# TensorE's side and softplus steps ahead of the sum, in every unit of a state-space scan kernel

## The chip, the cores and the metric

One NeuronCore of a Trainium2 chip runs the whole program in one launch. The metric is device time in microseconds, from the start of the execution to its end; lower is better.

## The reference

The program is four layers of a two-dimensional selective scan ("ss2d") over x of shape (8, 48, 48, 96), each as `x = x + layer(group_norm(x))`. All layers have 192 inner channels, 16 states, four scan directions k, and L = 48 * 48 = 2304 positions. Cut to what matters here:

```python
xc, z = split(x @ in_proj_w.T)                    # 192 + 192 channels
xc = silu(depthwise_conv3x3(xc) + conv_b)
xs = [rows, columns, rows reversed, columns reversed] of xc
dts, Bs, Cs = split(einsum('bkdl,kcd->bkcl', xs, x_proj_w))
delta = softplus(dts @ dt_projs_w + bias)
# per direction and channel d, along l:
h = h * exp(delta * A[d, n]) + (delta * u) * B[n]     # 16 states n
y[d] = sum_n h[n] * C[n]
y = sum of the four directions, brought back to rows, + D * xs
y = layer_norm(y) * silu(z);  out = y @ out_proj_w.T
```

Layers 0 to 2 are this recurrence. Layer 3 is written in the reference as a cumulative sum with a decay and an epsilon; the kernel has a shorter path for it.

## The kernel before, in words

The batch is taken in four pairs of images. For each layer and pair there is a **prologue** (group norm, projection, convolution, the projections that give dt, B and C), a **scan** over 36 chunks, and an **epilogue** (layer norm, gate, output projection, residual). The epilogue of the pair before and the prologue of the pair after are cut into small *side steps* and run beside the scan.

A **chunk** is 768 positions of one of three channel tiles t, one of two layouts ph and one direction d. It is worked through in 16 **units**, one for each n; a unit holds two states of 64 channels, one on each half of the 128 partitions. Layers 0 to 2 have 3 * 4 * 36 * 16 = 6,912 units. What one unit n costs on each engine:

- SyncE's queue loads the row C of the state, spread over partitions, into `cb` (line 740, 9 buffers), four units ahead; for "pooled" states (n = 2, 5, 7, 10, 13, 15) also B into `bb` (3 buffers), five ahead.
- TensorE spreads B over the partitions into PSUM (`b`, line 678, 2 buffers) for the states that are not pooled. It does this for state n + 1 in unit n.
- ScalarE makes the decay `da = exp(dl * a)` (line 780), three units ahead, or for a pooled state into the PSUM buffer `b`, one ahead.
- VectorE multiplies `b` by `du` (line 810, not for pooled states) and scans (line 814).
- GpSimd multiplies the scan by C into `cb` (line 823) and, for pooled states, B by `du` (line 757), three units ahead.
- TensorE adds the products up over the states into `acc` (line 870). In unit n the *sum* of state n - 2 is issued (`LAG` = 2): the sum of an odd state waits for GpSimd's product of that state, the sum of an even state needs nothing newer. The last sum of a chunk falls into unit 2 of the next chunk; ScalarE then copies `acc` to `y` (`collect`, line 887) at the head of unit 3, and the first sum of the new chunk (`begin_sum`, line 855) waits for that copy. One chunk in six passes its `acc` on and isn't copied.

Beside the units runs `prepare`, the **softplus step** for the next chunk: delta = softplus(...) and `du` in two halves of 384 positions. It is a generator that `beside()` moves by one step per unit: in unit 15 of the chunk before (second half: unit 6) TensorE's dt matmuls (line 614); in 0 (7) ScalarE's Abs, Relu, Exp (lines 622 to 624); in 1 (8) Ln and two Identity (626 to 628); in 2 (9) and in 3 (10) eight TensorE matmuls each, which add up the parts (line 634); then in 4 (11) ScalarE's four copies to `dl` (line 589) and VectorE's product with u (642, 645; in unit 4 for the first half, in 12 for the second), and in 5 (13) four copies to `du` (589).

The order of each engine's instructions in layers 0 to 2 is the order in which the program writes them (`keep_order`). Engines wait for one another by semaphores. In unit n the program writes:

```python
busy = collected()          # ScalarE: y <- acc, if a sum ended in the unit before
get_ready(k + 1)            # loads; B of n + 1; decay of n + 3
catch_up()
c.scan(n)
...
if busy and l not in short:
    beside()                # softplus's step, one side step (none in unit 2)
... b.add_up(bn)            # the sum of state n - 2
if not (busy and l not in short):
    beside()
```

So before the change `beside()` stands ahead of the sum only in the 360 units 3 that begin with a copy of `acc`.

Of the kernel before, what the change touches and what calls it, by code (L numbers as in the profile page):

```python
# [103 lines left out]
def ss2d_layers_kernel(ctx: ExitStack, tc: tile.TileContext, x_in, consts, weights, out):  # L104
# [470 lines left out]
    def load_dt(c):  # L575
        r = layers[c.l].rank
        c.dts = sm1.tile([64, SCAN], F32, name="dts", tag="dts")
        for b in c.batches:
            q0 = 32 * b if c.t == 2 else 0
            nc.sync.dma_start(  # L580
                c.dts[q0 : q0 + r, : c.m],
                state[c.l, c.p]["xd"][c.ph, b, c.d * r : (c.d + 1) * r, c.c0 : c.c0 + c.m],
            )
# [101 lines left out]
    def store_some(n):  # L685
        for _ in range(min(n, len(late_stores))):
            o, z, at = late_stores.pop(0)
            nc.sync.dma_start(o[:, at], z[:, at])

    def collected():  # L690
        some = bool(late_sums)
        while late_sums:
            late_sums.pop(0)()
        return some

    def catch_up():
        while late_act:
            nc.scalar.copy(*late_act.pop(0))
# [450 lines left out]
    def drain(g):  # L1149
        for _ in g:  # L1150
            pass

    def step(g):
        next(g, None)
# [7 lines left out]
    def side_step(*sides):  # L1162

        for s in sorted(sides, key=lambda s: (not s.held, s.made / s.total)):
            got = next(s.g, s)
            s.held = got is True
            if got is not s and got is not GATED:
                s.made += 1
                return True
        return False  # L1170
# [3 lines left out]
    def mark():  # L1174
        marks.append(len(tc._region_blocks()[0].instructions))
# [15 lines left out]
    def run(pairs, short):  # L1191


        def units():
            for l, p in pairs:
                for gi, (t, ph, d) in enumerate(groups):
                    if l in short:
                        c = Edge(l, p, t, ph, d)
                        for i in range(NS // QUAD):
                            yield (l, p, gi * (NS // QUAD) + i), c, i  # L1200
                        continue
                    group = {}
                    for i in range(len(SCANS)):
                        c = Chunk(l, p, t, ph, d, i, group, c if d == 1 and i == 0 else None)
                        for n in range(NS):
                            yield (l, p, (gi * len(SCANS) + i) * NS + n), c, n

        def begin(l, p, first=False):
            if l not in layers:
                layers[l] = Layer(l)  # L1210
            return prologue(l, p, l in short, first)

        todo = list(units())

        def rest_of_sum(k):
            before = todo[k - 1][1] if k > 0 else None
            if isinstance(before, Chunk) and (k == len(todo) or todo[k][1] is not before):
                before.add_up(NS)

        def get_ready(k):  # L1220

            def early(ahead, what):
                for i in range(0 if k == 0 else k + ahead, min(k + ahead + 1, len(todo))):
                    getattr(todo[i][1], what)(todo[i][2])

            early(LOADS + 1, "load_b")
            early(LOADS, "load")
            if k == 0:
                todo[0][1].decay(todo[0][2])
            if k < len(todo):  # L1230
                (l, p, _), c, n = todo[k]
                if n == 0 and c.first and l not in short:
                    c.group["carry"] = capool.tile([P, NS], F32, name="carry", tag="carry")
                c.spread(n)
            early(DECAYS, "weigh")
            for i in range(k + DECAYS if k else 1, min(k + DECAYS + 1, len(todo))):
                todo[i][1].decay(todo[i][2])

        rest = begin(*pairs[0], first=True)
        while next(rest) is not READY:  # L1240
            pass
        rest = Side(rest)
        chunks = list(dict.fromkeys(c for _, c, _ in todo))
        drain(prepare(chunks[0]))
        behind = ahead = Side()
        coming = iter(())
        done = None
        mark()
        get_ready(0)
        for k, ((l, p, unit), c, n) in enumerate(todo):  # L1250
            at = pairs.index((l, p))
            following = pairs[at + 1] if at + 1 < len(pairs) else None
            if l in short and unit == 0:
                mark()
            per = NS // QUAD if l in short else NS
            all_units = len(groups) * (per if l in short else len(SCANS) * per)
            place["tiles"] = 3 * unit // all_units
            store_some(1)
            if done:
                behind, done = Side(epilogue(*done), 199), None  # L1260
            if unit == LAG and following:
                ahead = Side(begin(*following), 311)
            if k == 0:
                coming_to = 1
                coming = prepare(chunks[coming_to])
            if n == max(0, per - 1 - DECAYS):
                while coming_to < len(chunks) and not chunks[coming_to].ready:
                    next(coming)
            if n == 10 and coming_to + 1 < len(chunks):
                z = chunks[coming_to + 1]  # L1270
                if (z.l, z.p) == (l, p):
                    load_dt(z)
            busy = collected()
            get_ready(k + 1)
            catch_up()
            c.scan(n)
            if n == per - 1:
                drain(coming)
                if unit + 1 + per == all_units:
                    drain(behind.g)  # L1280
                    drain(ahead.g)
                coming_to = chunks.index(c) + 2
                coming = prepare(chunks[coming_to]) if coming_to < len(chunks) else iter(())


            def beside():
                step(coming)

                for _ in range(10 if l in short else 0 if ends else 1):
                    side_step(rest) or side_step(behind, ahead)  # L1290

            ends = l not in short and k > LAG and todo[k - LAG][2] == 0
            if busy and l not in short:
                beside()
            if k >= LAG:
                (bl, bp, _), b, bn = todo[k - LAG]
                rest_of_sum(k - LAG)
                if bl in short:
                    collected()
                b.add_up(bn)  # L1300
                if k > LAG and todo[k - LAG - 1][0][:2] != (bl, bp):
                    done = todo[k - LAG - 1][0][:2]
            if not (busy and l not in short):
                beside()
        for i in range(len(todo) - LAG, len(todo)):
            collected()
            rest_of_sum(i)
            todo[i][1].add_up(todo[i][2])
            catch_up()
        collected()  # L1310
        rest_of_sum(len(todo))
        collected()
        drain(epilogue(*pairs[-1]))

    last = NLAYER - 1
    run([(l, p) for l in range(NLAYER) for p in range(NPAIR)], (last,))

    keep_order(*marks[:2])
# [8 lines left out]
    with tc.If(nc.values_load(again, min_val=0, max_val=1) > 0):  # L1327
        run([(last, p) for p in range(NPAIR)], ())
# [95 lines left out]
```

## Time and profile before

| | |
|---|---|
| runs (median; lowest to highest) | 20210.51 us; 20204.88 to 20238.13 us (3 runs) |
| profiled execution | 20200.44 us; span of its instructions 20198.6 us; mean granted TensorE clock 0.908 |
| layers 0 to 2 | 0 to about 18,304 us of the span |
| layer 3 (short path) | about 18,304 to 20,198 us |
| busy in the whole span | PE 83%, VectorE (DVE) 87%, ScalarE (ACT) 80%, GpSimd (POOL) 88%, DMA queue 79% of 16 engines |
| busy in 5,000 to 6,000 us | PE 858, DVE 935, ACT 835, POOL 947 of 1000 us |
| one matmul of a sum, 128x384 f32 | 486 ns median; four records for one sum |
| one scan, 128x768 | 1,814 ns (`da`, with carry); one product on GpSimd 1,817 ns; one product on VectorE 946 ns |

How to read it: times are microseconds of one profiled execution unless marked ns. PE is TensorE's matmuls, PEld its weight loads, SPq the queue that issues DMAs. In a list of waits, "A <- B: x, n" says that A's engine sat idle for x us in all, n times, until B released it. In the timeline a line gives the start, the length, the engine, the source line, the tiles, and in brackets the idle time of the engine before it and who ended it. "issue" is idle time that the profile puts to nobody. VectorE and GpSimd are the fullest engines, and neither is full: the profile has to be read by who waits for whom.

### The profile page before, as it was taken

The numbers are of one execution on the slowest core, as the hardware profiler recorded it, in microseconds if no ns is written. First come the engines' busy times: TensorE is split into PE (matmuls) and PEld (weight loads), VectorE is DVE, ScalarE is ACT, GpSimd is POOL, SyncE is SP. The second block draws the span as 40 slices with busy tenths as digits, with TensorE's granted clock in tenths as the row PEclk, the third lists the DMA queues.
The fourth block names the chain that finished last, engine by engine and source line by source line (L and its number), as shares of the span: only waits on it lengthen the run. The fifth ranks groups of instructions, "written<-read, shape, count | busy, mean of one in ns | idle before, by whom it ended". The sixth has DMA issues, their size and how long they took to land.

```text
span 20198.6 us, 314848 instructions
## 1 busy us (share of the span) xinstructions
PE 16790.8 (83%) x92962; PEld 7792.6 (39%) x92962; DVE 17667.0 (87%) x14161; ACT 16224.6 (80%) x30014; POOL 17769.4 (88%) x10121
## 2 busy tenths in 40 slices
PE   7888887887888888888887888888888887888886
PEld 3333333333333333333333333333333333334565
DVE  6999998998999999999999999999999999996553
ACT  6777887887887887887887887877877887887786
POOL 6999999999999999999999999999999999995442
PEclk9998998998998998998998999998999998999997
DMA  5888888888888888888888888888888888884221
GB/s 157 231 224 223 226 222 221 227 223 220 225 226 224 224 231 224 223 228 223 225 228 223 223 225 226 223 226 221 221 224 222 222 225 221 220 222 117 79 74 50
DMA packets 2021150, 4200.80 MB, mean 208 GB/s; under 512 B 375920, under 2 KB 789360, under 8 KB 2017904
## 3 DMA queue, kind: packets, MB, share of 16 engines
q1 hardware_dynamic: 2019440, 4180.55, 79.2%
q8 instruction: 762, 12.48, 0.3%
q14 instruction: 948, 7.77, 0.2%
HBM read 4026.64 MB, written 152.27 MB: 207 GB/s over the span
## 4 chain that ended last, share of the span: by engine, by line
PE 21%; ACT 17%; DVE 14%; DMA 10%; issue 9%; POOL 3%; SPq 2%; DVEq 0%; POOLq 0%; ACTq 0%
DVE da L814 7%; PE acc L870 5%; PE ps L634 4%; DMA bb<-xd 4%; DVE b L810 4%; DMA cb<-xd 4%; ACT b L780 3%; ACT dl L589 3%; PE ps L314 2%; PE b L678 2%; ACT du L589 2%; POOL cb L823 2%; DVE bb L814 2%; ACT da L780 2%; SPq L740 1%
## 5 line engine op out<-in xcount | busy, mean ns | idle before, releaser
L823 POOL TENSOR_TENSOR cb<-cb,da 128x768 f32<-128x768 f32 x4320 | 7835.9, 1819 | 749.3 <-issue 253.1
L870 PE MATMUL acc<-cb,twin 128*64 128x384 f32 x27648 | 7200.8, 539 | 721.3 <-POOL cb L823 704.5
L814 DVE TENSOR_TENSOR_SCAN da<-da,carry,b 128x768 f32<-128x768 f32 x2880 | 5223.2, 1814 | 176.0 <-DVE b L810 0.9
L757 POOL TENSOR_TENSOR bb<-bb,du 128x768 f32<-128x768 f32 x2592 | 4716.9, 1820 | 222.2 <-DMA bb<-xd 125.6
L823 POOL TENSOR_TENSOR cb<-cb,bb 128x768 f32<-128x768 f32 x2592 | 4706.8, 1816 | 100.2 <-DVE bb L814 50.7
L810 DVE TENSOR_TENSOR b<-du,b 128x768 f32<-128x768 f32 x4320 | 4085.6, 946 | 690.2 <-PE b L678 604.2
L678 PE MATMUL b<-brow,pick 96*64 96x512 bf16 (+2 forms) x18816 | 2852.5, 353 | 1886.2 <-DVE da L814 1528.4
L780 ACT ACTIVATE da<-dl,a 128x768 f32<-128x768 f32 x4320 | 4011.3, 930 | 213.5 <-POOL cb L823 183.0
L870 PEld LDWEIGHTS acc<-cb,twin 128*64 128x64 f32 x27648 | 2452.5, 149 | 2998.4 <-POOL cb L823 1333.5
L814 DVE TENSOR_TENSOR_SCAN bb<-b,carry,bb 128x768 f32<-128x768 f32 x1728 | 3109.6, 1800 | 106.0 <-ACT b L780 35.6
L780 ACT ACTIVATE b<-dl,a 128x768 f32<-128x768 f32 x2592 | 2335.3, 901 | 623.2 <-DVE da L814 598.4
L678 PEld LDWEIGHTS <-pick 96*64 96x64 bf16 x18816 | 1077.9, 115 | 4164.4 <-DVE da L814 2717.6
L814 DVE TENSOR_TENSOR_SCAN da<-da,b 128x768 f32<-128x768 f32 x1440 | 2525.3, 1754 | 87.4 <-DVE b L810 1.4
L314 PE MATMUL ps<-pad,diag 128*64 128x480 f32 (+1 forms) x8640 | 2339.7, 567 | 34.6 <-ACT du L589 24.4
L589 ACT COPY dl<-ps 64x384 f32<-64x384 f32 x3456 | 1632.6, 472 | 697.9 <-PE ps L634 659.6
L589 ACT COPY du<-ps 64x384 f32<-64x384 f32 x3456 | 1633.5, 473 | 200.7 <-DVE ps L645 109.8
L634 PE MATMUL ps<-du,cst 128*64 128x384 f32 (+1 forms) x7296 | 1704.5, 506 | 76.5 <-ACT du L628 65.6
L814 DVE TENSOR_TENSOR_SCAN bb<-b,bb 128x768 f32<-128x768 f32 x864 | 1502.1, 1739 | 145.5 <-ACT b L780 92.2
L634 PE MATMUL ps<-dl,cst 128*64 128x384 f32 (+1 forms) x7296 | 1485.2, 483 | 0.0
L614 PE MATMUL ps<-dts,w 6*128 6x384 f32 (+5 forms) x2432 | 961.4, 605 | 205.0 <-DMA dts<-xd 105.4
L622 ACT ACTIVATE du<-ps,w 128x384 f32<-128x384 f32 (+1 forms) x912 | 519.9, 570 | 714.6 <-PE ps L614 701.0
L314 PEld LDWEIGHTS ps<-pad,diag 128*64 128x64 f32 x8640 | 751.8, 139 | 885.0 <-issue 729.6
(144 smaller groups left out, 19166.4 us busy)
## 6 DMA issues: line engine op xcount, KB each, us to landing
cb<-xd SPq DMA_DIRECT2D x13952, 192.0 KB
bb<-xd SPq DMA_DIRECT2D x5184, 192.0 KB
brow<-xb SPq DMA_DIRECT2D x864, 72.0 KB
ey<-yd SPq DMA_DIRECT2D x256, 216.0 KB
cb<-xd SPq DMA_DIRECT2D x128, 384.0 KB
yd<-y SPq DMA_DIRECT2D x216, 192.0 KB
ex<-xs SPq DMA_DIRECT2D x256, 108.0 KB
xb<-parts SPq DMA_DIRECT2D x96, 216.0 KB
```

The source lines that it names most:

```text
L314: nc.tensor.matmul(ps[half, :m], ly.diag[:, int(t == 2), j, half], pad[:, r0 + dy : r0 + dy + nr, dx : dx + W], start=(j == 0), stop=(j == 8),
L589: nc.scalar.copy(z[64 * h : 64 * h + 64, g, at], v[64 * g : 64 * g + 64])
L614: nc.tensor.matmul(o[:, :m], ly.dtw[q0 : q0 + r, k, chans], dts[q0 : q0 + r, at], start=True, stop=True,)
L622: nc.scalar.activation(e, v, AF.Abs, bias=bias)
L634: nc.tensor.matmul(v[half], ident[:, half], z1, start=(i == 0), stop=(i == 3))
L678: nc.tensor.matmul(o[64 * h : 64 * h + 64], pick[:, b, n : n + 1].to_broadcast([2 * NR, 64]), rows, start=True, stop=True,)
L757: nc.gpsimd.tensor_mul(b, b, self.du[n % 2])
L780: nc.scalar.activation(da, self.dl[n % 2], AF.Exp, scale=layers[self.l].a2[:, int(self.t == 2), n % 2, k, i : i + 1],)
L810: nc.vector.tensor_mul(b, self.du[n % 2], b)
L814: nc.vector.tensor_tensor_scan(way(h), way(da), way(b), start, ALU.mult, ALU.add)
L823: nc.gpsimd.tensor_mul(c, c, h)
L870: nc.tensor.matmul(self.acc[64 * g : 64 * g + 64, a, : self.m // 2], twin, c[:, a, :], start=False, stop=(pair + 2 == NS and not self.turns),)
```

## The change

In layers 0 to 2, `beside()` stands ahead of the sum in every unit, behind the next B; for layer 3's short path it stays behind the sum. No instruction is added or removed.

```diff
-            busy = collected()
+            collected()
             get_ready(k + 1)
             catch_up()
             c.scan(n)
...
-            if busy and l not in short:
+            if l not in short:
                 beside()
             if k >= LAG:
...
                 b.add_up(bn)
...
-            if not (busy and l not in short):
+            if l in short:
                 beside()
```

## The prediction

> **What bounds the kernel now.** I read the page first, then the list of waits, then the timeline of two spots, and last the granted clock in short windows.
>
> The chain that ended last, from the page, names no single engine, so the end is set by hand-overs:
>
> ```profile
> PE 21%; ACT 17%; DVE 14%; DMA 10%; issue 9%; POOL 3%; SPq 2%; DVEq 0%; POOLq 0%; ACTq 0%
> ```
>
> From the list of waits, the rows that the change can reach (who waits <- for whom: us in all, times, longest):
>
> ```profile
> PEld acc L870 <- POOL cb L823: 1333.5, 1033, 4.6
> ...
> ACT du L622 <- PE ps L614: 701.0, 395, 12.2
> ACT dl L589 <- PE ps L634: 659.6, 411, 4.7
> DVE b L810 <- PE b L678: 604.2, 623, 10.5
> ...
> ACT y L887 <- PE acc L870: 250.8, 250, 5.2
> ...
> POOL bb L757 <- DMA bb<-xd: 125.6, 107, 4.0
> ```
>
> and from the list of SyncE's queue:
>
> ```profile
> SPq L740 <- PE acc L870: 1862.4, 1719, 6.5
> ```
>
> TensorE waits for GpSimd in front of a sum; ScalarE waits for the softplus matmuls that stand behind sums; VectorE waits for B. VectorE is the pacemaker: it waits almost never for GpSimd, and what it loses is to B (604 us) and to ScalarE. So I price everything as VectorE's idle time. To place it I number the 6,912 scans of the trace by start, sixteen to a chunk. Of the 604 us, 264 fall before state 1, 180 before state 11 (201 waits), 64 before state 6, 58 before state 12, 49 before 0, 43 before 3, the rest elsewhere.
>
> The first spot is unit 9 of one chunk:
>
> ```profile
> 12438.84 0.62 ACT L628 ACTIVATE du<-du,ones 128x384 f32<-128x384 f32 x1
> ...
> 12441.61 0.54 PE L870 MATMUL acc<-cb,twin 128*64 128x384 f32 x1 [2.22 <-POOL cb L823]
> ...
> 12441.99 1.77 PE L634 MATMUL ps<-du,cst 128*64 128x384 f32 x7
> ...
> 12444.87 0.52 PE L678 MATMUL b<-brow,pick 96*64 96x512 bf16 x4
> ...
> 12445.43 0.96 DVE L810 TENSOR_TENSOR b<-du,b 128x768 f32<-128x768 f32 x1 [1.36 <-PE b L678]
> ```
>
> TensorE idles 2.22 us for the product of state 7, though the softplus matmuls behind it were ready at 12439.46, and the B of state 11 comes 1.36 us late.
>
> The second spot is units 2 to 4 of another chunk:
>
> ```profile
> 5305.49 0.81 PE L870 MATMUL acc<-cb,twin 128*64 128x384 f32 x4
> ...
> 5306.14 1.46 PE L634 MATMUL ps<-du,cst 128*64 128x384 f32 x8
> ...
> 5306.38 0.80 ACT L887 COPY y<-acc 128x768 f32<-128x768 f32 x1 [0.61 <-PE acc L870]
> ...
> 5309.53 0.91 ACT L780 ACTIVATE b<-dl,a 128x768 f32<-128x768 f32 x1 [0.95 <-DVE da L814]
> ...
> 5310.45 1.93 ACT L589 COPY dl<-ps 64x384 f32<-64x384 f32 x4
> ...
> 5312.41 0.57 DVE L642 TENSOR_TENSOR ps<-ps,u 128x384 f32<-128x384 f32 x1
> ```
>
> Here the order of before serves ScalarE: the last sum ends, and the copy of `acc` goes at once.
>
> **The change part by part.** No instruction comes or goes. `add_up` issues matmuls alone, so the order on ScalarE, VectorE, GpSimd and SyncE's queue stays as it is, the side steps' DMAs included; only TensorE's order changes. A sum is 0.64 us of TensorE (four matmuls at the 0.16 us by which they follow one another in the second spot), a softplus step 1.29 us (eight).
>
> *Unit 9, gain.* In the example the eight softplus matmuls would run from 12439.5 and take the same 2.14 us, the side step 1.25 us to 12442.9, the sum to 12443.5, B to 12444.1; VectorE is free at 12444.06. The wait of 1.36 us is gone. The same sum over 429 chunks (softplus step at the later of TensorE's last end and the end of L628; then the side step; the sum at the later of that and the product's end) leaves 17 us of lateness before state 11 where it gives 155 for the old order. I take 150 of the 180 us.
>
> *Unit 10, gain.* TensorE comes 0.8 us earlier out of unit 9, and most of the 165 waits before state 12 (58 us, 0.35 each) are shorter than that: 40 us.
>
> *ScalarE's waits.* L622 and L589 wait 1,361 us for matmuls that now come a sum (0.64 us) or more earlier. ScalarE is 80% busy, and the pooled states' scans wait 128 us for it in all; most of those waits stand behind table loads and long copies that nothing here moves. I take 15 us, from 0 to 35.
>
> *Unit 2, loss.* The chunk's last sum now stands behind eight softplus matmuls, 1.29 us. Who waits: L887, at the head of ScalarE's queue, and behind it the decay, the `b` of state 5, the copies to `dl`, and VectorE's product with u behind those. In the example the copy of `acc` moves from 5306.38 to 5307.67; the decay (0.94) and a side step's copy (0.56) follow, L780 starts at 9.97 instead of 9.53, and `dl` ends at 12.82 instead of 12.38: VectorE starts at 12.83, 0.4 us late. Over the 355 such chunks that I could follow, the same sum gives 219 us, of which 64 replace waits for the B of state 6: some 150 us. From the other side: sort the chunks by when that copy ends after scan 1, and the wait for `dl` grows from 0.13 us (2.8 us after) to 0.25 (3.8): 0.12 us on 360 chunks, 45 us. I take 140, nearer to the direct sum; the ends are 45 and 219.
>
> *Held side steps, loss.* In 356 units TensorE waits inside a side or softplus step (22 of them L614 for its `dts` load, over 0.3 us each in unit 15). A sum used to fill part of that time and now stands behind it. At 0.64 us each it is 228 us of TensorE; followed to the B behind, 38 us reach VectorE. I take 35, from 0 to 100.
>
> *Loads, loss.* `cb` comes free with the sum, and SyncE's queue already waits 1,862 us for it. A `cb` is asked for 12.9 us before its use (median), so later by one step costs nothing there; but `bb` loads stand behind in the queue, are asked for 7.3 to 7.7 us before use in most states, and GpSimd waits 126 us for them. Only state 13's follows a unit with a long step (6) closely. I take 15 us, from 0 to 50.
>
> *Clock.* The pause that unit 9 loses doesn't vanish: TensorE has the same work, and the idle time moves in front of the B of states 14 and 0, where it already averages 1.1 and 2.0 us. What such a pause does shows in four windows around a state 0 (the first numbers are PE's busy us, the column before the last two the granted clock):
>
> ```profile
> 4392.53:4395.94 3.41, 0.56 (x6) 0.44 (x8) 3.38 (x4) 3.33 (x8) 3.41 (x3) 1.00 0.88 203
> 4395.94:4399.35 3.41, 3.41 (x10) 0.62 (x6) 3.37 (x3) 1.59 (x4) 2.68 (x2) 0.50 0.65 202
> ```
>
> After a window with PE busy for 0.56 us the clock is halved. I cut the whole trace into these windows: at full clock, 274 of 275 with PE busy below 40% were followed by half clock, 53% of those between 40 and 50%, none above 80%. The B of state 1 is late by 0.94 us on average where the clock was mostly halved (260 chunks), by 0.10 elsewhere (168). If 30 chunks more fall into half clock there, that is 25 us; the ends are 140 us (all 168 at 0.84) and a gain of 70 (a halved clock filling the pause earlier, and 84 chunks fewer at state 1). The Trainium skill weighs this otherwise: "TensorE: Matmul & The Clock Gate", section "What's actually happening", halves the clock after an idle window of about 3.4 us. By that rule a longer pause of 2 to 3 us costs nothing and the sum would be 25 us lower; the windows above, halved after one that was 40 to 50% busy, speak against it.
>
> **Sum.** -150 - 40 - 15 + 140 + 35 + 15 + 25 = +10 us on the profiled execution of 20200.4, so 20,210; the median of the runs shown lies 10 us above it, so 20,220. A measurement of this kernel can tell about 0.2%, 40 us, from no change.
>
> **The rivals.**
>
> *Balance, within 80 us of before* (forecast, 20,220): relief in units 9 and 10 is paid back in unit 2 and in held steps. For: both prices are near 200 us, each from rows. Against: they are independent. 42%.
>
> *The relief wins.* ScalarE has slack behind unit 3 (it waits for scans before `b`, 0.95 us in the second spot), so the later copy costs only the 45 us, and steps held cost nothing: -205 + 45 + 15 = -145 us, 20,065. For: in most chunks ScalarE waits at L780. Against: it must then make `dl` late by less than a quarter of what the row gives. 27%.
>
> *The late copy wins (slower).* In unit 2 the sum behind 1.29 us of softplus makes ScalarE late for `dl` in unit 4, VectorE loses the whole 219 us, and the pause moved to state 0 adds 75 us of half clock, held steps 60; B gives back only 150: +204 us, 20,415. It decides once the copies to `dl` move by more than 0.5 us per chunk. For: VectorE reaches L642 0.14 us after scan 4 already. 31%.
>
> *TensorE's order doesn't matter,* since it idles 17% anyway: then ScalarE's 1,361 us shrink and the time stays. It is part of the balance.
>
> **How the numbers follow.** Of the balance's 42%, 10 lie under -40 us, 18 within, 14 above. Faster 0.10 + 0.27 = 0.37; same 0.18; slower 0.14 + 0.31 = 0.45. The balance's own range is 20,130 to 20,290. For 8 in 10 the range reaches to the relief's value and near to the late copy's: 20,060 to 20,400.
>
> **What would show it.** Right: the wait of L870 for L823 falls from 1,333 us to a third or less; L589's for L634 by 400 us or more; L887's for L870 rises from 251 to 500 or more; VectorE's wait before state 11 falls under 50 us, its wait for `dl` before L642 and L645 rises from 125 us to over 200. Wrong: these waits move and VectorE's idle sum falls or rises by over 200 us; or L887 waits no longer than now; or the half clock share before state 1 (61%) changes by over 20 points, and with it the 264 us.

## The result: slower by 0.64%

| | before | after |
|---|---|---|
| runs, median (lowest to highest) | 20207.69 us (20188.39 to 20238.13, 6 runs) | 20348.44 us (20311.84 to 20364.55, 6 runs) |
| profiled execution | 20200.44 us, clock 0.908 | 20359.95 us, clock 0.904 |

The ratio is 1.0064, interval [1.0054, 1.0075]: about 130 us more. The forecast (20,220) had the time unchanged; its range, 20,060 to 20,400, holds the result because it was stretched towards the slower rival's 20,415; the sum itself said +10 us.

### The profile after

The chain that ended last still names no single engine, but DMA's share of it has grown from 10% to 13%:

```profile
PE 20%; ACT 18%; DMA 13%; DVE 13%; issue 8%; SPq 3%; POOL 1%; DVEq 0%; POOLq 0%; ACTq 0%
```

The list of waits of the changed kernel (who waits <- for whom: us in all, times, longest):

```profile
ACT y L887 <- PE acc L870: 841.9, 348, 6.6
PEld acc L870 <- POOL cb L823: 812.0, 961, 3.9
DVE b L810 <- PE b L678: 720.5, 536, 11.6
...
ACT du L622 <- PE ps L614: 521.9, 265, 12.0
...
PEld ps L614 <- ACT du L589: 433.6, 324, 6.1
...
PE b L678 <- DMA brow<-xb: 358.0, 123, 8.1
...
POOL bb L757 <- DMA bb<-xd: 244.4, 205, 4.3
...
DVE ps L642 <- ACT dl L589: 221.4, 171, 75.4
PE ps L614 <- ACT du L589: 219.0, 208, 5.4
...
ACT dl L589 <- PE ps L634: 167.6, 160, 4.4
DVE ps L645 <- ACT dl L589: 160.1, 192, 5.3
```

The first rows are as foretold: TensorE's wait for GpSimd ahead of a sum shrinks (1333.5 to 812.0), so does ScalarE's for the softplus matmuls (659.6 to 167.6), and ScalarE's for the last sum grows (250.8 to 841.9). VectorE's waits for `dl` grow too; L645's was 62.6 us before, and L642's row of before is:

```profile
DVE ps L642 <- ACT dl L589: 131.1, 100, 81.5
```

Its longest wait, 75 to 82 us at the very start of the program, stands in this row of every run. The rows on loads are the surprise. TensorE waits 358.0 us for `brow`, the chunk's B; the same row of before, which the prediction did not look at, reads:

```profile
PE b L678 <- DMA brow<-xb: 154.9, 45, 5.9
```

SyncE's queue, which issues these loads, waits longer for TensorE: its two largest rows "SPq L740 <- PE" sum to 3,185 us, where they were 2,319 (1862.4, shown with the prediction, and 456.8). First the row of before that was not shown, then the two of the changed kernel:

```profile
SPq L740 <- PE b L678: 456.8, 749, 6.8
```

```profile
SPq L740 <- PE b L678: 1755.2, 1323, 8.1
SPq L740 <- PE acc L870: 1430.0, 1119, 9.4
```

The two spots of the prediction, in the same chunks, show both main steps at work. First unit 9, in the timeline (start, length, engine, line, tiles, in brackets idle time and who ended it):

```profile
12555.60 0.62 ACT L628 ACTIVATE du<-du,ones 128x384 f32<-128x384 f32 x1
...
12556.27 0.87 PE L634 MATMUL ps<-du,cst 128*64 128x384 f32 x4 [0.26 <-ACT du L628]
...
12558.24 1.17 PE L870 MATMUL acc<-cb,twin 128*64 128x384 f32 x3
...
12559.57 0.49 PE L678 MATMUL b<-brow,pick 96*64 96x512 bf16 x2
...
12560.74 0.94 DVE L810 TENSOR_TENSOR b<-du,b 128x768 f32<-128x768 f32 x1
```

The softplus matmuls start right behind L628, B ends at 12560.06, and VectorE's product shows no wait where it had 1.36 us. Then units 2 to 4:

```profile
5380.09 1.46 PE L634 MATMUL ps<-du,cst 128*64 128x384 f32 x8
...
5381.38 0.81 PE L870 MATMUL acc<-cb,twin 128*64 128x384 f32 x4
...
5382.26 0.80 ACT L887 COPY y<-acc 128x768 f32<-128x768 f32 x1 [3.49 <-PE acc L870]
...
5384.37 0.90 ACT L780 ACTIVATE b<-dl,a 128x768 f32<-128x768 f32 x1
5385.28 1.93 ACT L589 COPY dl<-ps 64x384 f32<-64x384 f32 x4
...
5387.24 0.57 DVE L642 TENSOR_TENSOR ps<-ps,u 128x384 f32<-128x384 f32 x1 [0.36 <-ACT dl L589]
```

The sum now follows the eight softplus matmuls, ScalarE stands idle for 3.49 us before its copy, and VectorE is 0.36 us late for `dl`, against 0.4 foretold for this chunk.

### Where VectorE's time went

VectorE paces the scan, so I keep a ledger of it: the time from the end of one scan to the end of the next, averaged by state, times the 432 chunks, less the same of before (us; one profile of each kernel, so a few us are noise; states that never move by over 15 are left out). The columns on the right are the experiments below.

| state | after | all but 2 | all but 10 | early brow | only 9 | only 2 | only 6 | all but 2, 6 |
|---|---|---|---|---|---|---|---|---|
| 0 | +60 | +51 | +63 | -10 | +25 | +1 | +7 | +60 |
| 1 | +102 | +69 | +62 | +1 | +60 | +3 | +32 | +69 |
| 3 and 4 | +15 | +9 | -4 | +45 | -1 | +16 | +27 | +5 |
| 5 (wait for `dl`) | +179 | -21 | +157 | +193 | +8 | +223 | +7 | -21 |
| 6 | -46 | +2 | -47 | -45 | 0 | -46 | +8 | -6 |
| 8 | +56 | +47 | +61 | +47 | -6 | +5 | +35 | +2 |
| 11 | -126 | -116 | -133 | -115 | -127 | -49 | +9 | -98 |
| 12 | -59 | -53 | -61 | -60 | -61 | -9 | -1 | -59 |
| all 16 | +160 | -30 | +98 | +40 | -105 | +150 | +112 | -58 |

The gains stand in states 11 and 12, the losses in 5, in 8, and in 0 and 1, where the prediction expected 15 us for loads and 25 for the clock.

### The profile page after: what moved, and what is told of

The parts are those of the page before. It is cut to its first block, busy times and chain, and to the rows that moved or that the text cites. A ratio compares the mean times of both kernels' runs of the same rounds, so it can differ in the third digit from the quotient of the medians.

```text
span 20358.1 us, 314830 instructions
## 1 busy us (share of the span) xinstructions
PE 16780.1 (82%) x92962; PEld 7592.2 (37%) x92962; DVE 17638.6 (87%) x14161; ACT 16244.1 (80%) x30014; POOL 17766.8 (87%) x10121
## 4 chain that ended last, share of the span: by engine, by line
PE 20%; ACT 18%; DMA 13%; DVE 13%; issue 8%; SPq 3%; POOL 1%; DVEq 0%; POOLq 0%; ACTq 0%
DVE da L814 6%; DMA cb<-xd 5%; DMA bb<-xd 5%; PE acc L870 5%; DVE b L810 3%; ACT b L780 3%; PE ps L634 3%; ACT da L780 3%; PE ps L314 3%; ACT dl L589 3%; PE b L678 2%; DMA brow<-xb 2%; ACT du L589 2%; SPq L740 2%; DVE bb L814 2%
## 5 line engine op out<-in xcount | busy, mean ns | idle before, releaser
L823 POOL TENSOR_TENSOR cb<-cb,da 128x768 f32<-128x768 f32 x4320 | 7831.1, 1818 | 704.2 <-issue 251.8
L870 PE MATMUL acc<-cb,twin 128*64 128x384 f32 x27648 | 6946.9, 543 | 283.1 <-POOL cb L823 267.4
L757 POOL TENSOR_TENSOR bb<-bb,du 128x768 f32<-128x768 f32 x2592 | 4716.8, 1820 | 441.8 <-DMA bb<-xd 244.4
L823 POOL TENSOR_TENSOR cb<-cb,bb 128x768 f32<-128x768 f32 x2592 | 4713.6, 1819 | 87.7 <-DVE bb L814 37.2
L810 DVE TENSOR_TENSOR b<-du,b 128x768 f32<-128x768 f32 x4320 | 4077.7, 944 | 727.9 <-PE b L678 720.5
L678 PE MATMUL b<-brow,pick 96*64 96x256 bf16 (+2 forms) x18816 | 2739.8, 353 | 1943.5 <-DVE da L814 1447.8
L870 PEld LDWEIGHTS acc<-cb,twin 128*64 128x64 f32 x27648 | 2280.2, 149 | 3296.3 <-issue 2209.0
L678 PEld LDWEIGHTS <-pick 96*64 96x64 bf16 x18816 | 1116.5, 118 | 4350.4 <-DVE da L814 2705.7
L314 PE MATMUL ps<-pad,diag 128*64 128x480 f32 (+1 forms) x8640 | 2118.9, 571 | 42.6 <-ACT du L589 27.0
L589 ACT COPY du<-ps 64x384 f32<-64x384 f32 x3456 | 1633.3, 473 | 293.3 <-DVE ps L645 154.8
L589 ACT COPY dl<-ps 64x384 f32<-64x384 f32 x3456 | 1632.4, 472 | 205.5 <-PE ps L634 167.6
L634 PE MATMUL ps<-du,cst 128*64 128x384 f32 (+1 forms) x7296 | 1527.9, 508 | 260.0 <-ACT du L628 243.2
L634 PE MATMUL ps<-dl,cst 128*64 128x384 f32 (+1 forms) x7296 | 1398.0, 483 | 0.0
L887 ACT COPY y<-acc 128x768 f32<-128x768 f32 x360 | 416.7, 1157 | 852.4 <-PE acc L870 841.9
```

The source lines that it names most:

```text
L314: nc.tensor.matmul(ps[half, :m], ly.diag[:, int(t == 2), j, half], pad[:, r0 + dy : r0 + dy + nr, dx : dx + W], start=(j == 0), stop=(j == 8),
L589: nc.scalar.copy(z[64 * h : 64 * h + 64, g, at], v[64 * g : 64 * g + 64])
L634: nc.tensor.matmul(v[half], ident[:, half], z1, start=(i == 0), stop=(i == 3))
L678: nc.tensor.matmul(o[64 * h : 64 * h + 64], pick[:, b, n : n + 1].to_broadcast([2 * NR, 64]), rows, start=True, stop=True,)
L757: nc.gpsimd.tensor_mul(b, b, self.du[n % 2])
L810: nc.vector.tensor_mul(b, self.du[n % 2], b)
```

## The experiments

The theories: A, the late copy of `acc` in unit 2 is the loss; B, loads come late because `cb` comes free later, `brow` among them; C, it is the half clock behind TensorE's pauses. Later expectations use the letters for narrower forms, and say which. All ratios are against before, on the same chip, in five rounds; 0.0001 is 2 us. Except where shown, the edits differ in one condition alone:

```diff
-            if l not in short:
+            front = l not in short and (CONDITION)
+            if front:
                 beside()
...
-            if l in short:
+            if not front:
                 beside()
```

Where `busy` stands in a condition, it keeps before's order in unit 3.

### All units but 2

```diff
+ CONDITION: n != 2
```

> The change in every unit but 2, where the sum of the chunk's last state stays ahead of the softplus step. From the two traces, VectorE's period by state: state 5 longer by 0.41 us (its product with u waits for ScalarE's copies to dl), state 6 shorter by 0.11. Theory A (late copy of acc): that is 130 us of the loss and goes: about 20,215 us, ScalarE's wait for acc before L887 back to about 250 us, the wait for dl before L642 and L645 back to about 130. Theory B (late loads: the whole loss comes from SyncE's queue, held by sums): stays within 30 us of 20,348.

Measured: 20174.29 us, 0.9993 [0.9983, 1.0002]. Unit 2 carries 0.71%, some 143 us; its state 5 goes from +179 to -21. The list of waits:

```profile
ACT y L887 <- PE acc L870: 361.0, 278, 5.6
...
DVE ps L642 <- ACT dl L589: 123.4, 95, 81.7
```

The first has gone most of the way back to before's 250.8, the second the whole way (131.1). The time fell further than A's figure: A was right in kind and a little too low in size.

### All units but 10

```diff
+ CONDITION: n != 10
```

> The change in every unit but 10, where the sum stays ahead of eight softplus matmuls. From the two traces, states 0 and 1 are longer by 0.14 and 0.23 us after the change (160 us in all). Theory B (late loads: the sum of unit 10 frees the cb that SyncE's queue waits for in unit 11, the load of brow, L765, stands behind it, and state 0's B waits for brow): the waits for brow fall from 358 us back towards 150, states 0 and 1 get 100 to 160 us back, state 12 loses up to 40: 20,200 to 20,290 us. Theory C (clock: TensorE, earlier since unit 9, pauses longer before state 0's B and runs at half clock at state 1): stays within 40 us of 20,348.

Measured: 20298.56 us, 1.0048 [1.0035, 1.0062]. The interval overlaps that of the full change, and the median lies between the two expectations: inconclusive on the time. Theory B's own sign did not come: TensorE's wait for `brow` stays at 343.8 us, and states 0 and 1 keep 125 of their 162 us, so the sum of unit 10 alone is not what makes `brow` late. The ledger says one more thing clearly: state 12 gains 61 us without unit 10's edit, so that gain belongs to unit 9, out of which TensorE comes earlier.

### The full change with an early brow

`brow` is issued in unit 12 of the chunk before: behind the `cb` of state 15 (unit 11), which waits for the sum of unit 10, and ahead of the `cb` of state 0, on the same queue. Here it is issued one unit earlier, ahead of the `cb` of state 15:

```diff
         def load_b(self, n):
+            if n == 0:
+                s, m, at = state[self.l, self.p], self.m, slice(self.c0, self.c0 + self.m)
+                self.brow = rpool.tile([2 * NR, SCAN], BF16, name="brow", tag="brow")
+                for j, b in enumerate(range(2) if self.t == 2 else (self.t, self.t)):
+                    nc.sync.dma_start(
+                        self.brow[NR * j : NR * j + NR, :m],
+                        s["xb"][self.ph, b, :, self.d, :, at],
+                    )
             if not self.pooled(n):
...
-            if n == 0:
-                self.brow = rpool.tile([2 * NR, SCAN], BF16, name="brow", tag="brow")
...
             self.cb[n] = cb
```

> The change in full, and brow of the next chunk is loaded one unit earlier, in front of the cb that waits for the sum of unit 10. Theory B (late loads): state 0's wait for B falls from 114 us to 50 or less and state 1's from 363 towards 264: 20,190 to 20,270 us. Theory C (clock): state 1's wait stays over 340, at most the 65 us of state 0 come back: 20,280 to 20,350.

Measured: 20247.17 us, 1.0027 [1.0016, 1.0037]: 75 us of the loss came back. The wait for the load falls to a quarter (list of waits):

```profile
PE b L678 <- DMA brow<-xb: 89.4, 26, 5.8
```

and the losses of states 0 and 1 go, +162 to -9. Some of that returns as 30 us more in states 3 and 4. GpSimd's wait for `bb` falls as well (244.4 to 154.7), so a part of the 75 us may lie there. How `brow` came to be late: its issue lies 1.78 us behind the end of scan 10 before, 2.97 us after, 0.5 us here (medians of 428 chunks). The load itself is no slower: where TensorE waits for `brow`, it goes on 6.4 us (median) after the end of the issue before and 6.3 us after the change. What shrank is the lead, from the end of the issue to TensorE's first use, from 7.9 to 6.4 us (medians of 431 chunks). The Trainium skill, "DMA: Bandwidth & Descriptors", section "Anatomy of one DMA — SWDGE (gpsimd) path", says that a semaphore wait happens on the issuing sequencer before dispatch. It describes DMAs that GpSimd issues; for SyncE's, the rows "SPq L740 <- PE" above agree, and once `brow` stands ahead of a `cb` load that waits, TensorE waits for it 26 times instead of 123: that `cb` load held what stood behind it.

What a late `brow` costs shows in one chunk of the changed kernel:

```profile
7291.78 0.59 SPq L740 DMA_DIRECT2D cb<-xd  x1
...
7292.42 1.53 SPq L765 DMA_DIRECT2D brow<-xb  x2
...
7301.75 0.52 PE L678 MATMUL b<-brow,pick 96*64 96x512 bf16 x4 [1.70 <-DMA brow<-xb]
...
7302.30 0.96 DVE L810 TENSOR_TENSOR b<-du,b 128x768 f32<-128x768 f32 x1 [0.95 <-PE b L678]
...
7305.54 1.55 PE L870 MATMUL acc<-cb,twin 128*64 128x384 f32 x4
...
7306.87 0.85 PE L678 MATMUL b<-brow,pick 96*64 96x512 bf16 x4
...
7307.77 0.96 DVE L810 TENSOR_TENSOR b<-du,b 128x768 f32<-128x768 f32 x1 [2.72 <-PE b L678]
```

and in the busy times by window (PE first; the granted clock is the third column from the end):

```profile
7299.17:7302.58 3.41, 1.71 (x14) 0.50 (x10) 2.46 (x3) 1.42 (x3) 1.81 (x1) 1.00 0.74 185
7302.58:7305.99 3.41, 3.41 (x14) 2.24 (x12) 2.43 (x2) 2.53 (x6) 1.91 (x2) 0.50 0.74 220
```

TensorE waits 1.70 us for the load, B of state 0 is 0.95 us late, and the clock is then halved: the next sum takes 1.55 us instead of 0.81, and B of state 1 is 2.72 us late. So B and C are one chain here. Count the chunks whose B of state 0 starts over 0.3 us behind the end of scan 14: 63 before, 147 after, 57 with the early load. VectorE's wait before state 1 is 47, 148 and 42 us in those, and 214, 210 and 220 us in all others: what the change adds there stands wholly behind a late `brow`.

### Unit 9 alone

```diff
+ CONDITION: busy or n == 9
```

> The order of before, and the softplus step and side step ahead of the sum in unit 9 alone (besides the units 3 that had it before). If the relief is what the two traces show by state (state 11 -0.29 us, state 12 -0.14 on 432 chunks) and unit 9's sum, of an odd state, frees no cb: 180 us less than before at best, about 20,050 us. If the relief was only room that GpSimd or the clock takes back elsewhere: 20,190 to 20,220 us.

Measured: 20097.97 us, 0.9948 [0.9934, 0.9962]. Faster than both kernels, by 105 us against before, between the two expectations. States 11 and 12 give 188 us, states 0 and 1 take 85 back.

### Unit 9 alone, with the early brow

The two edits together.

> The step goes ahead of the sum in unit 9 alone (and in unit 3's copies, as before), and the chunk's `brow` load is issued one unit earlier, ahead of the `cb` loads that wait. The run with unit 9 alone took 96 us less than before, while its states 0 and 1 cost 25 and 60 us more of VectorE's period than before. Theory B (states 0 and 1 suffer from the late `brow`): the 85 us go and some 40 of the 49 + 264 us that before already lost there go too: about 20,000, from 19,970 to 20,040. Theory C (states 0 and 1 suffer from the half clock that follows TensorE's pause, wherever it lies): the early load only moves the pause; 20,070 to 20,110.

Measured: 20072.13 us, 0.9942 [0.9928, 0.9955]. The early load takes off another 12 us, which the intervals do not tell from nothing: B's figure is wrong for this order, and C's is met. But C's cause is not seen: the chunks with half clock before state 1 fall from 260 of 428 before to 214. State 1 keeps +50 us, in chunks whose `brow` was in time (214 to 270 us); why its B is later there stays open.

### Before, with the early brow

> A control: TensorE's order is that of before, only the `brow` load is issued one unit earlier. Theory B (a late `brow` already costs before): the 78 us that B of state 0 waits for `brow` in 44 chunks shrink by most, and with them part of state 1's: 50 to 95 us less, 20,110 to 20,150. Rival (the load is late only because the change puts the sum later): within 30 us of before, 20,170 to 20,230; then the 101 us that the early load saved in the changed order belong wholly to the change.

Measured: 20174.36 us, 0.9990 [0.9981, 0.9999]. 20 us: the rival. States 0 and 1 gain 49, states 3 and 4 lose 26. So of the 75 us that the early load saves in the full change, some 55 are the change's own.

### Unit 2 alone

```diff
+ CONDITION: busy or n == 2
```

> The step goes ahead of the sum in unit 2 alone (and in unit 3's copies, as before). Theory A (unit 2 alone makes ScalarE's copy of `acc` late, and with it the copies to `dl` and VectorE's product with u): 135 to 175 us more than before, 20,330 to 20,370; VectorE's wait for `dl` at lines 642 and 645 rises by over 150 us. Rival (the price of unit 2 comes about only together with unit 9, since VectorE then reaches the product with u sooner): under 80 us, below 20,275.

Measured: 20348.13 us, 1.0073 [1.0059, 1.0086]: 147 us, theory A, and the same as the price of its removal (143). The list of waits:

```profile
ACT y L887 <- PE acc L870: 736.6, 347, 7.1
...
ACT dl L589 <- PE ps L634: 598.0, 390, 4.4
...
DVE ps L642 <- ACT dl L589: 243.8, 170, 75.4
...
DVE ps L645 <- ACT dl L589: 180.7, 190, 5.3
```

### All but 2 and 6, with the early brow

```diff
+ CONDITION: n not in (2, 6), with the early load
```

> The step goes ahead of the sum in every unit but 2 and 6, with the early `brow` load. Theory A (states 8's 47 us, held by the dt matmuls of unit 6 that wait for ScalarE's copies, go with unit 6; the units other than 9 and 10 bring nothing): about as the run with unit 9 and the early load, less 0 to 60 us for unit 10, so 19,950 to 20,040. Rival (the other units' steps hold sums up as well, and GpSimd's `cb` come free later): 20,060 to 20,110, near the run without unit 2 less the early load's gain.

Measured: 20072.80 us, 0.9941 [0.9927, 0.9954]. That is the rival's figure, but A's statement: unit 9 with the early load took 20,072 us, not the 20,000 that A's figure started from, and this run took the same. With the load early, the other 13 units bring nothing and cost nothing. State 8's loss is gone with unit 6 (+7).

### All units but 6

```diff
+ CONDITION: n != 6
```

> The changed order in every unit but 6, where the dt matmuls of the second half (line 614) stay behind the sum. Theory B (the dt matmuls wait there for ScalarE's copies to `du`; ahead of the sum they hold it, and the Bs up to state 8's, up): VectorE's loss before state 8, 56 us more than before the change, goes, so 20,290 to 20,320. Rival (unit 6 is worth nothing; what the units other than 2 and 9 cost lies in the late `brow` alone): within 25 us of the changed kernel, 20,325 to 20,375.

Measured: 20259.44 us, 1.0029 [1.0018, 1.0040], below both figures: unit 6 carries 0.35%, 71 us, more than the 56 that stood before state 8, of which 7 are left.

### Unit 6 alone

```diff
+ CONDITION: busy or n == 6
```

> The step goes ahead of the sum in unit 6 alone (and in unit 3's copies, as before). Theory B (unit 6 costs by itself): 30 to 60 us more than before, 20,225 to 20,260, all of it in front of state 8. Rival (the hold only costs where unit 2 has already made ScalarE's copies late): under 20 us, below 20,220; then the run without unit 2, which kept 47 us in front of state 8, has to be explained otherwise.

Measured: 20316.88 us, 1.0058 [1.0044, 1.0072]: 117 us, twice the most that theory B said, and only 35 of them before state 8. The list of waits has the mechanism; line 614's wait for the copies at L589 sums to 507 us (before, the rows are 225.3 and 86.3), and the loads wait more too (154.9 and 125.6 before):

```profile
PEld ps L614 <- ACT du L589: 339.0, 258, 5.0
...
PE b L678 <- DMA brow<-xb: 229.8, 75, 7.3
...
POOL bb L757 <- DMA bb<-xd: 181.9, 143, 5.3
...
PE ps L614 <- ACT du L589: 168.1, 155, 4.7
```

The dt matmuls need a PSUM bank that ScalarE is still copying from. Ahead of the sum, they hold up the sum, the `cb` that it frees, and the loads behind that `cb`.

### Unit 6 alone, with the early brow

> The step goes ahead of the sum in unit 6 alone, with the early `brow` load. The run with unit 6 alone cost 117 us: some 35 in front of state 8, some 70 in front of states 0 to 4. Theory B (the 70 us are loads that SyncE's queue issues later, since `cb` comes free later): with the early load states 0 and 1 lose their 39 us and the 20 us that the load is worth by itself; 1.002 to 1.004 times before, about 20,250. Rival (they are half clock behind TensorE's longer pause in unit 6): 1.0045 to 1.006, 20,295 to 20,325.

Measured: 20266.61 us, 1.0031 [1.0019, 1.0042], theory B: the early load takes 55 us off, where it took 20 off before. The wait for it:

```profile
PE b L678 <- DMA brow<-xb: 74.1, 23, 5.9
```

So of unit 6's 117 us, some 35 are a `brow` that unit 6 makes late, 35 to 39 are state 8's B, and the rest, spread over states 3, 4, 6 and 11, I cannot place.

### All but 2 and 6, loads as before

```diff
+ CONDITION: n not in (2, 6)
```

> The changed order in every unit but 2 and 6, loads as before. Theory B (units 2, 6 and 9 carry the whole; the other 13 bring nothing): within 0.0015 of the 0.9948 of unit 9 alone, 20,070 to 20,130. Rival (the other 13 make the loads late too, as the 75 us show that the early load saved in the full change): 0.9965 to 0.9985, 20,130 to 20,175.

Measured: 20149.97 us, 0.9970 [0.9961, 0.9980]: the rival. Beside unit 9 alone, the other 13 units cost 0.22%, 44 us, and with the early load they cost nothing (0.9941 against 0.9942). The row behind it:

```profile
PE b L678 <- DMA brow<-xb: 274.6, 91, 7.7
```

With unit 9 alone it is 194.2. Each of these steps puts the sum, and with it `cb` and the queue, further back. Which of the 13 carry the 44 us is not shown; unit 10 is a candidate (without it the full change took 0.16% less), but there the intervals overlap.

### The account

Unit 9 alone -105, unit 2 alone +147, unit 6 alone +117, the other 13 together +44: +203 us, where the full change costs 130. The single prices overlap: taken out of the full change, unit 6 is worth 71, not 117. The ledger shows where. In states 0 and 1, where a late `brow` is paid, the columns "only 2", "only 6" and "all but 2, 6" add up to what the full change has (68 and 104 against 60 and 102). In states 3 and 4 and in state 5 they add up to more (48 and 209 against 15 and 179); why stays open. With the prices of removal for units 2 and 6, -105 + 143 + 71 + 44 = 153; the 23 us left are within what these intervals can tell. Four of these orders are clearly faster than both kernels (0.9941 to 0.9970). The best, unit 9 with the early load and all but 2 and 6 with it, stand at 0.9942 and 0.9941, some 120 us under before, and cannot be told apart.

## Why the prediction was right or wrong

**Unit 9 (-150): right in kind, a little too high.** The ledger has -126 in the full change and -127 with unit 9 alone. 73 us of waiting are left before state 11, not under 50. The wait of before was read loosely: the parts given for the 604 us add up to 658, since of the 178 us before state 11 only 102 are in the row "DVE b L810 <- PE b L678"; the trace puts the other 76 to the sum, `PE acc L870`. That unit 9 alone makes states 0 and 1 dearer by 85 us has only the 25 us of the clock for it in the sum.

**Unit 10 (-40): right, and for the reason given.** -59, which unit 9 brings alone (-61).

**Unit 2 (+140): right, from its own chain.** The ledger has +179 in state 5 less 46 in state 6; the runs say 143 and 147. In the 359 chunks behind a copy of `acc`, the copies to `dl` end 0.57 us later on average, just over the 0.5 us from which the slower rival was to decide. The lower end, 45 us from the sorted chunks, was the poorer guide, perhaps because it compared chunks that were late for other reasons.

**ScalarE's waits (-15): not seen.** L589's wait for L634 fell by 492 us, and VectorE's waits for ScalarE in the pooled scans did not fall (127.8 to 135.3 us).

**Held steps (+35): the size of one part, not of all.** State 8 alone pays 56. The term followed the hold to the next B and stopped there; unit 6 costs 71 to 117, and of the 117 some 35 are loads that the held sum holds up.

**Loads (+15, at most 50): the step that failed.** It listed `cb` and `bb` as what stands in SyncE's queue, and left out `brow`, which is issued behind a `cb`, once a chunk, 7.9 us (median) ahead of its use, where a load that TensorE waited for took 6.4. In before's list of waits it was a row of 154.9 us already. It is worth some 55 us by the early load, and states 0 and 1 together lose 162 in the ledger.

**Clock (+25): right in kind, wrong in cause.** Chunks with half clock before state 1 went only from 260 to 278 of 428, but B is 1.28 us late in them on average instead of 0.94, and the added waiting stands in chunks with a late `brow`. In the full change, the pause that mattered was made by a load, not by the one that unit 9 gave up. The window that the prediction shows was such a case already: the pause ahead of its 0.56 us ends with

```profile
4395.38 0.52 PE L678 MATMUL b<-brow,pick 96*64 96x512 bf16 x4 [3.37 <-DMA brow<-xb]
```

So it did not show what the idle time in front of state 0 does in general. With a pause of 3.37 us it also fits the idle window of about 3.4 us that the prediction weighs there, and does not speak against it; the windows that were 40 to 50% busy do. Counted over the whole trace of before, at full clock 309 of 309 windows below 40% were followed by half clock, 127 of 233 between 40 and 50%, and 2 of 3,059 above 80%, both in layer 3: other counts than the prediction's, the same reading.

By the ledger -126 - 59 - 46 + 179 + 56 + 162 = 166 of the 160 us. The first four make -52, close to the prediction's -50 for units 9, 10 and 2; the error sits in the last two, state 8 and states 0 and 1, 218 us where the prediction had 35 + 15 + 25. So the forecast case, the balance, did not come about: what units 9, 10 and 2 left even, the loads and unit 6 tipped. The slower rival had the sign, and the point from which it decides, but its place only in part: unit 2 did not cost 219 us but 143, and loads and unit 6 made up for it. Of the signs, VectorE's idle sum in layers 0 to 2 rose by 181 us (1,529 to 1,710), under the 200 named, and L870's wait for L823 fell by 39%, not to a third; the waits of L589 and L887 and those for `dl` moved as foretold.

## What to carry to other kernels

When an instruction that frees a buffer is moved back, write down everything that stands behind that buffer's refill in the same DMA queue, the rare loads too, and how far ahead of their use they are issued; a load with little lead is the one that pays. Move a step ahead of another only where the step is ready, the one that it passes still waits for something, and nobody waits for that one: here one unit in sixteen, unit 9, had all of the gain, and unit 2, where ScalarE waits for the sum that is passed, lost by itself as much as the whole change did. A hand-written order is cheap to try unit by unit, but the prices of single units add up only roughly: 203 us here, where the whole took 130.

## What the hardware showed that I had not expected

A longest pause of 1.70 us was enough for a halved clock. The windows above show it: TensorE was busy for 1.71 of 3.41 us, and the clock stood at 0.50 for the 6.8 us that followed. Of the 636 stretches at half clock in this trace 323 last 3.41 us and 198 twice that, so I cut the trace into windows of 3.41 us that begin where the clock changes. At full clock, 327 had PE busy below 40%, and all were followed by half clock; so were 121 of 195 between 40 and 50%, 98 of 333 between 50 and 60%, and 4 of 3,049 above 80% (3 of the 4 in layer 3). The way back is dearer: of the windows at half clock with PE busy below 70%, none was followed by full clock, and of 882 above 80% 629 were. The Trainium skill, "TensorE: Matmul & The Clock Gate", section "What's actually happening", names an idle window of about 3.4 us as what throttles; the length agrees with these rows, but the window need not be idle: here it was half busy.
